# Layer 1's normalised batches turned by VectorE and DMAs instead of TensorE

## The chip, the core and the metric

The kernel runs on one core of one Trainium2 chip. Its engines work side by side, each through its own list of instructions in order: TensorE (PE in the profile; its weight loads are PEld) multiplies matrices into PSUM, VectorE (DVE), ScalarE (ACT) and GpSimd (POOL) work elementwise, SyncE (SP) issues most DMAs. An instruction that must wait for another engine or for a DMA waits on a semaphore, and everything behind it on its own engine waits with it. The metric is the device time of one execution in microseconds (us). Three runs of the kernel before gave 2046.7, 2047.1 and 2048.27.

## The reference, cut to what matters

The program computes two transformer layers on x of shape (4, 512, 512), each an attention and a feed-forward part (FFN) behind a layernorm that is scaled and shifted per batch. Layer 1, which the change concerns:

```python
h = _layernorm(x, axis=-1) * (1 + ca) + sa
x = x + ga * _L1_attn_ref(h, w_q, w_k, w_v, w_o)     # 32 heads of 128, 8 kv heads, causal
h = _layernorm(x, axis=-1) * (1 + cb) + sb
x = x + gb * _L1_ffn_ref(h, ...)                     # down(silu(gate(h)) * up(h)), 1792 wide, int weights with scales
```

`sa, ca, ga, sb, cb, gb` come from a small matrix product of a conditioning vector, one row per batch. The matmuls of both parts sum over the 512 features, and TensorE sums over partitions. The layernorm sums over features too, but is done with rows of x on the partitions. So the normalised x (rows on partitions) must be turned into h with features on partitions before it can be used. How it is turned is what the change is about.

## The kernel before, in words

Everything is fp32 or fp32r (P = 128, NT = 4 tiles of 128 rows a batch, KC = 4 chunks of 128 features, B = 4 batches, HKV = 8).

*Layer 0* comes first and is not touched. It ends near 205 us of the span.

*Attention of layer 1* runs over 32 blocks n, eight (g = 0 to 7) for each batch b. A block is two windows (`window`, lines 1120 to 1149), each with the scores, softmax and transposes of the eight tiles of the next pair of heads, the value products of the present pair, and a list of pieces, `fill`, which are dealt out over nine slots: products of the q, k, v and output projections, each as seven quarter products (`seven`, line 738). Two more lists, `side`, hold small work for the same slots. The order on every engine is written out by hand: what is issued first in the code stands first on its engine. `carry` (line 911) moves turned probabilities between partitions with 16 DMAs at the end of each window, on SP's queue; the value products read them in slots 8 and 9 of the next window.

A batch's x rests in DRAM (`x_d`). For the next batch (`after`) it is loaded in the odd window of block g = 4 into the one buffer `one_x`, and normalised in the even window of g = 5 by `norm_pieces` (line 995): VectorE takes the statistics, GpSimd the power -1/2 (`rstd`), VectorE `nmr`, and ScalarE scales the rows in place. In the odd window `turn_pieces` (line 1026) has TensorE turn four 128x128 squares a chunk into a PSUM bank (`lnT`, line 1035), and ScalarE scales, shifts and writes h1 (line 1038). Four empty pieces stand in the `fill` list of every odd window where a block has no turns (line 1263). `sums_h` then makes sums of h1 on GpSimd. The four h buffers `hp` hold h1 and its sums for two batches.

*The FFN* (`ffn_exact`, line 1281) runs over 4 batches of 14 steps n. In a step, `hidden` (line 1341) has TensorE compute gate and up (eight matmuls of 512 columns each, p_gate and p_up, line 1349), ScalarE take the sigmoid (line 1355), VectorE two products (1356, 1357), ScalarE the rounded half act_hi (122) and VectorE the rest act_lo (123). `down` (line 1363) then multiplies the halves of the step before into four accumulators (line 1368). Weights come in seven blocks, each of a gate, an up and a down part: `load` (line 1330) has SP load them into three rotating buffers wi and GpSimd cast them (line 1338), one block every second step of the first batch. The first batch also finishes what attention left: seven sums on GpSimd, four gates on VectorE (line 965) and four adds on GpSimd (line 969), three pieces a step from step 1 on. At step 8 the rows gb are loaded (`gates`, line 1051).

`prepare` (line 1294) makes the next batch's h in pieces, one a step from step 2: four statistics, the deviation (`ve`, `rstd`, `nmr`; line 63), two pieces of two normalised rows each (line 1306; into the room of attention's accumulator osum, called acc in the profile), and in steps 9 to 12 the four chunks: four transposes on TensorE into the bank `lnT` (line 1314), a scaling by VectorE (1318), and the two halves. The first batch's own h is made by `split_pieces` in attention's last windows, on TensorE.

[...]

Every DMA signals one of eight completion semaphores. They are given out in turn over all DMAs, whichever queue issues them, and a DMA isn't issued before the previous one on its semaphore has landed.

Of the kernel before, what the change touches and what calls it, by code (L numbers as in the profile page):

```python
# [8 lines left out]
F32 = mybir.dt.float32  # L9
# [8 lines left out]
P = 128  # L18
# [15 lines left out]
def adaln_two_layers(ctx: ExitStack, tc: tile.TileContext, a, out: bass.AP):  # L34
# [960 lines left out]
    def norm_pieces(xb):  # L995
# [7 lines left out]
        def xn(t):  # L1003
            nc.scalar.activation(
                xb[:, t, :], xb[:, t, :], AF.Identity,
# [19 lines left out]

    def turn_pieces(b, got):
# [3 lines left out]
        def piece(c):  # L1030
            if c == 0:
                h1[b] = hp.tile([P, KC, S], F32, tag="hT", name="hT")
            pt = bank([P, S], "lnT")
            for t in range(NT):
                nc.tensor.transpose(  # L1035
                    pt[:, t * P : (t + 1) * P], got["xn"][:, t, c * P : (c + 1) * P], ident
                )
# [4 lines left out]
            if c == KC - 1:  # L1042
                sums_h(b, (nc.gpsimd, nc.gpsimd))

        return [lambda c=c: piece(c) for c in range(KC)]
# [131 lines left out]
    begun = []  # L1177

    for n in range(NBLK):
# [17 lines left out]
        if g == HKV - 4:  # L1197
            xb = one_x()
            side[1] = get(after, xb)
        if g == HKV - 3 and after or n == NBLK - 2:  # L1200
            got, side[0] = norm_pieces(xb)
            if after:
                turns_ = turn_pieces(after, got)
# [12 lines left out]
        elif ahead:  # L1216
# [3 lines left out]
            else:  # L1220
                window(2 * n, begun[:2] + q[:2] + begun[2:] + q[2:], side[0], late)
                begun = []
                if 2 * (m + 1) < NBLK:
# [34 lines left out]
        else:  # L1258
# [4 lines left out]
            more = turns_ + 4 * [lambda: None]  # L1263
            window(2 * n + 1, o[:3] + now + more[:1] + o[3:4] + more[1:2] + o[4:5] + more[2:3] + o[5:6] + more[3:4] + o[6:], side[1], late)
# [16 lines left out]
    def ffn_exact():  # L1281
        with (
# [5 lines left out]
            tc.tile_pool(name="ps_tr2", bufs=1, space=PSUM) as ps_tr2,  # L1288
            tc.tile_pool(name="ps_hu", bufs=3, space=PSUM) as ps_hu,
# [4 lines left out]
            def prepare(b):  # L1294
# [3 lines left out]
                xn = osum.rearrange("p a b c -> p (a b c)")[:, : NT * E]  # L1298
                xn = xn.rearrange("p (t e) -> p t e", e=E)
# [4 lines left out]
                def norm(t):  # L1304
                    rstd, nmr = d["dev"]
                    nc.scalar.activation(
                        xn[:, t, :], x[b][:, t, :], AF.Identity,
                        bias=nmr[:, t : t + 1], scale=rstd[:, t : t + 1],
                    )
# [189 lines left out]
```

## Time and profile before

| what | value |
|---|---|
| three runs | 2046.7, 2047.1, 2048.27 us |
| profiled execution | 2046.79 us, of which the span from the first to the last instruction 2044.8 us |
| mean granted TensorE clock | 0.989 |
| TensorE busy | 2011.8 us, 98% |
| VectorE, ScalarE, GpSimd busy | 67%, 43%, 37% |
| TensorE waiting, all waits named | 1.8 us at most for any one cause after layer 0 but one (kT, 2.6 us) |
| first gate matmul of the FFN starts | 1727.53 us |

How to read it: the page gives busy time by engine; a group row has the line, engine, operation, tile written and tiles read, and durations. TensorE's durations contain a latency that the next matmul overlaps, so the distance of two starts is what a matmul costs. A wait row reads: engine, line that waited, what it waited for, total, times, longest. Rows in order of time begin with start and duration.

### The profile page before, as it was taken

The page shows a single profiled execution, that of the slowest core. Times are in us where ns is not written, and L with a number is a line of the kernel's source. Part 1 is how long each engine was busy: PE and PEld are TensorE (multiplying, and loading weights), DVE is VectorE, ACT ScalarE, POOL GpSimd, SP SyncE. Part 2 cuts the span into 40 slices and gives each one's busy share as a digit, 9 for nine tenths or more (in the row PEclk, how much of TensorE's full clock was granted, in tenths as well). Part 3 has the DMA queues.
Part 4 walks back from the last instruction along what each step waited for, and adds up shares of the span by engine and source line. Part 5 has one row for each costly group of instructions (what it writes and reads, how often), then busy time and mean ns, then how long its engine had stood idle before and what let it go on. Part 6 is the DMA issues. An engine that isn't in the chain of part 4 may idle for free.

```text
span 2044.8 us, 27496 instructions
## 1 busy us (share of the span) xinstructions
PE 2011.8 (98%) x9219; PEld 1573.9 (77%) x9219; DVE 1370.6 (67%) x3325; ACT 875.1 (43%) x1993; POOL 760.7 (37%) x659
## 2 busy tenths in 40 slices
PE   6999999999999999999999999999999999999998
PEld 4555777878787878777787878787877777888887
DVE  7767876677667766766677676667666675755554
ACT  4421644445444444544444445444444443323322
POOL 2316244334336433353473334337334333800000
PEclk8799999999999999999999999999999999999999
DMA  9222566665667766556776665567656556500000
GB/s 315 104 68 93 135 161 167 157 165 145 146 168 183 181 162 160 150 145 168 180 183 162 147 165 134 146 154 175 166 149 155 135 129 215 192 21 2 19 21 23
DMA packets 243640, 288.59 MB, mean 141 GB/s; under 512 B 23250, under 2 KB 184018, under 8 KB 243492
## 3 DMA queue, kind: packets, MB, share of 16 engines
q1 hardware_dynamic: 242964, 285.71, 53.2%
q8 instruction: 76, 1.25, 0.3%
q10 hardware_dynamic: 528, 1.05, 0.1%
q14 instruction: 72, 0.59, 0.1%
HBM read 142.99 MB, written 11.57 MB: 76 GB/s over the span
## 4 chain that ended last, share of the span: by engine, by line
PE 88%; DVE 1%; SPq 0%; DMA 0%; ACT 0%; issue 0%; DVEq 0%; ACTq 0%
PE quarter L746 46%; PE av L928 14%; PE sc L878 13%; PE p_gate L1349 5%; PE p_up L1349 5%; PE acc L1368 5%; PE lnT L1035 0%; PE lnT L1314 0%; DVE nmx L881 0%; SPq L918 0%; DMA x<-p 0%; DVE tm L1089 0%; DVE x L1377 0%; DVE tm L1376 0%; DVE p L896 0%
## 5 line engine op out<-in xcount | busy, mean ns | idle before, releaser
L878 PE MATMUL sc<-kT,qT 128*128 128x512 f32 (+3 forms) x1024 | 355.4, 433 | 0.8 <-DVE qT L778 0.8
L928 PE MATMUL av<-x,v 128*128 128x512 f32 x1008 | 292.1, 433 | 1.8 <-DMA x<-p 1.8
L928 PEld LDWEIGHTS av<-x,v 128*128 128x128 f32 x1008 | 188.4, 190 | 106.9 <-issue 62.4
L881 DVE TENSOR_REDUCE nmx<-sc 128x1 f32<-128x512 f32 (+3 forms) x512 | 251.6, 491 | 17.7
L893 ACT ACTIVATE x<-x,rden 128x512 f32<-128x512 f32 (+3 forms) x256 | 143.7, 561 | 239.3 <-DVE rden L892 239.3
L778 DVE TENSOR_TENSOR qT<-qT,quarter 128x512 f32<-128x512 f32 x224 | 150.6, 684 | 136.4 <-PE quarter L746 130.2
L893 ACT ACTIVATE p<-p,rden 128x512 f32<-128x512 f32 (+3 forms) x256 | 143.8, 562 | 223.2 <-DVE rden L892 221.7
L879 DVE TENSOR_TENSOR sc<-sc,mask 128x128 f32<-128x128 f32 x512 | 145.3, 284 | 133.1 <-PE sc L878 132.2
L842 DVE TENSOR_TENSOR acc<-acc,quarter 128x512 f32<-128x512 f32 x196 | 134.6, 687 | 131.4 <-PE quarter L746 131.3
L230 POOL TENSOR_TENSOR sq<-wq 128x512 f32<-128x512 f32 x32 | 41.1, 1286 | 474.0 <-DMA wq<-in_L_attn_w_q_dram 455.4
L878 PEld LDWEIGHTS sc<-kT,qT 128*128 128x128 f32 x1024 | 182.7, 191 | 25.5 <-DVE qT L778 1.2
L746 PEld LDWEIGHTS quarter<-wo,oT 128*128 128x128 f32 x744 | 140.9, 190 | 43.9 <-issue 20.1
L883 ACT ACTIVATE p<-sc,nmx 128x512 f32<-128x512 f32 (+3 forms) x256 | 135.1, 528 | 85.8 <-DVE nmx L881 77.2
L746 PE MATMUL quarter<-wo,oT 128*128 128x256 f32 x744 | 171.1, 379 | 0.2 <-ACT oT L933 0.2
L883 ACT ACTIVATE x<-sc,nmx 128x512 f32<-128x512 f32 (+3 forms) x256 | 134.9, 527 | 70.1 <-DVE nmx L881 65.4
L933 ACT COPY oT<-av 128x512 f32<-128x512 f32 x128 | 74.3, 580 | 162.1 <-PE av L928 160.2
L896 DVE STREAM_TRANSPOSE p<-p 128x512 f32<-128x512 f32 (+3 forms) x256 | 129.5, 506 | 1.8 <-ACT p L893 0.2
L896 DVE STREAM_TRANSPOSE x<-x 128x512 f32<-128x512 f32 x248 | 125.1, 504 | 1.4 <-ACT x L893 0.9
L746 PEld LDWEIGHTS quarter<-hT,wq 128*128 128x128 f32 x512 | 97.2, 190 | 32.5 <-issue 14.6
L746 PE MATMUL quarter<-hsum,sq 128*128 128x256 f32 x512 | 121.1, 379 | 0.0
L746 PE MATMUL quarter<-hsum,wq 128*128 128x256 f32 x512 | 121.0, 379 | 0.0
L746 PE MATMUL quarter<-hT,wq 128*128 128x256 f32 x512 | 120.9, 379 | 0.0
(257 smaller groups left out, 3749.4 us busy)
## 6 DMA issues: line engine op xcount, KB each, us to landing
x<-p SPq DMA_DIRECT2D x512, 128.0 KB, 3.7
x<-x SPq DMA_DIRECT2D x496, 128.0 KB, 3.8
wq<-in_L_attn_w_q_dram SPq DMA_DIRECT2D x32, 1024.0 KB, 5.9
wo<-in_L_attn_w_o_dram SPq DMA_DIRECT2D x31, 1024.0 KB, 5.6
wm<-in_L_wmod_dram SPq DMA_DIRECT2D x12, 1024.0 KB, 9.5
wk<-in_L_attn_w_k_dram SPq DMA_DIRECT2D x16, 512.0 KB, 4.0
wv<-in_L_attn_w_v_dram SPq DMA_DIRECT2D x16, 512.0 KB, 4.4
xn<-x_d SPq DMA_DIRECT2D x28, 256.0 KB, 5.6
```

The lines of the kernel that those rows point to most:

```text
L746: nc.tensor.matmul(ps[:, m, :], l[:, k, m * P : (m + 1) * P], r[:, k, :], start=(k == 0), stop=(k == 1),)
L778: nc.vector.tensor_tensor(c[out], c[v], ps, ADD if sign > 0 else SUB)
L842: nc.vector.tensor_tensor(osum[:, i - 1], osum[:, i - 1], ps, ADD)
L878: nc.tensor.matmul(ps[:, :w], q[:, i * P : w], kT[n][:, :w], start=True, stop=True)
L879: nc.vector.tensor_tensor(ps[:, i * P : w], ps[:, i * P : w], mask, ADD)
L881: nc.vector.tensor_reduce(nmx, ps[:, :w], AX.X, ALU.max, negate=True)
L883: nc.scalar.activation(blocks(s, i), ps[:, :w].rearrange("p (j q) -> p j q", q=BK), AF.Exp, bias=nmx, accum_out=den,)
L893: nc.scalar.mul(p, p, rden)
L896: nc.vector.transpose(blocks(s, i), blocks(s, i))
L928: nc.tensor.matmul(av.rearrange("p (a n) -> p a n", a=NG)[:, :, BK * k :], vs[n][:, k, :], pT[:, k, :, P * (s % 2) + BK * k : P * (s % 2 + ...
L1349: nc.tensor.matmul(ps[kind], w[kind][:, k, c * P : (c + 1) * P], h2[b % 2][i][:, k, :], start=(k == 0 and i == 0), stop=(k == KC - 1 and i ...
L1368: nc.tensor.matmul(acc[t], act[i][:, t * P : (t + 1) * P], w[:, c, :], start=(n == 0 and i == 0), stop=(n == NI - 1 and i == 1),)
```

## The change

In attention, for batches 1 to 3, the normalised rows are written in blocks of 32 columns (z, called xblocks), VectorE turns the 32x32 squares of such a block (four instructions of 512 columns a batch), and 16 DMAs on SP's queue move the turned squares to the partitions where they belong (y, called xturned), eight after the odd window of block g = 3, after its carry, and eight after the next even window. ScalarE then writes h1 from y. For this, x is loaded at g = 2 and normalised at g = 3. h1 is written in the odd window of g = 5, from the `side` list. The empty pieces in `fill` are gone. z and y use h buffers that are free at the time.

In the FFN, z and y lie in the room of osum. Two chunks are handled at a time (h = 0, 1): a normalised row is written in two halves, VectorE turns four blocks of 256 columns, and 16 DMAs for each half are issued by ScalarE, eight a step. Pieces begin at step 1, with two statistics a step. What attention left over is done at five pieces a step. The transposes' PSUM bank goes to gate and up. Layer 0 and the first FFN batch keep their transposes on TensorE.

```diff
+    TURN = [P, P // 32, NT, KC, 32]
+    def place_of(z, t):
+        return z[:, :, t], lambda ap: ap.rearrange("p (c j q) -> p j c q", j=P // 32, q=32)
+    def turn_blocks(z, j):
+        zj = z[:, j].rearrange("p t c q -> p (t c) q")
+        nc.vector.transpose(zj, zj)
+    def move_blocks(z, y, j, eng=nc.sync):
+        for i in range(P // 32):
+            eng.dma_start(y[32 * j : 32 * (j + 1), i], z[32 * i : 32 * (i + 1), j])
+    def chunk_of(y, c):
+        return y[:, :, :, c, :]
+    def in_order(ap):
+        return ap.rearrange("p (t i q) -> p i t q", t=NT, q=32)
...
     def turn_pieces(b, got):
-            pt = bank([P, S], "lnT")
-            for t in range(NT):
-                nc.tensor.transpose(
-                    pt[:, t * P : (t + 1) * P], got["xn"][:, t, c * P : (c + 1) * P], ident
-                )
             nc.scalar.activation(
-                h1[b][:, c, :], pt, AF.Identity,
+                in_order(h1[b][:, c, :]), chunk_of(got["y"], c), AF.Identity,
                 bias=m[:, 0, c, b : b + 1], scale=m[:, 1, c, b : b + 1],
             )
...
-        if g == HKV - 4:
+        if g == (HKV - 6 if after else HKV - 4):
             xb = one_x()
             side[1] = get(after, xb)
-        if g == HKV - 3 and after or n == NBLK - 2:
-            got, side[0] = norm_pieces(xb)
+        if g == HKV - 5 and after or n == NBLK - 2:
+            got, side[0] = norm_pieces(xb, after > 0)
             if after:
-                turns_ = turn_pieces(after, got)
+                turns_ = [lambda j=j: turn_blocks(got["z"], j) for j in range(P // 32)]
+        if g == HKV - 3 and after:
+            turns_ = turn_pieces(after, got)
...
+                run(*moves)
+                moves = []
...
-            more = turns_ + 4 * [lambda: None]
-            window(2 * n + 1, o[:3] + now + more[:1] + o[3:4] + more[1:2] + o[4:5] + more[2:3] + o[5:6] + more[3:4] + o[6:], side[1], late)
+            window(2 * n + 1, o[:3] + now + o[3:], turns_ + side[1], late)
+            if g == HKV - 5 and after:
+                moves = move_pieces(got)
+                run(moves.pop(0), moves.pop(0))
...
-            tc.tile_pool(name="ps_tr2", bufs=1, space=PSUM) as ps_tr2,
-            tc.tile_pool(name="ps_hu", bufs=3, space=PSUM) as ps_hu,
+            tc.tile_pool(name="ps_hu", bufs=4, space=PSUM) as ps_hu,
...
                 def norm(t):
                     rstd, nmr = d["dev"]
+                    for h in range(2):
+                        dst, read = place_of(z[:, h], t)
+                        nc.scalar.activation(
+                            dst, read(x[b][:, t, h * E // 2 : (h + 1) * E // 2]), AF.Identity,
+                            bias=nmr[:, t : t + 1], scale=rstd[:, t : t + 1],
+                        )
+                def turned_(h):
+                    for j in range(P // 32):
+                        turn_blocks(z[:, h], j)
+                def move(h, js):
+                    for j in js:
+                        move_blocks(z[:, h], y, j, nc.scalar)
                 def chunk(c):
+                    t = temp()
                     sc_, sh_ = m[:, 3, c, b : b + 1], m[:, 2, c, b : b + 1]
-                    nc.vector.tensor_scalar(t, pt, sc_, sh_, ALU.mult, ALU.add)
+                    nc.vector.tensor_scalar(
+                        in_order(t), chunk_of(y, c % 2), sc_, sh_, ALU.mult, ALU.add
+                    )
                     halves(h2[b % 2][0][:, c, :], h2[b % 2][1][:, c, :], t)
                 return (
-                    [lambda t=t: statistics(b, t, st, mv) for t in range(NT)] + [dev]
-                    + [lambda t=t: (norm(t), norm(t + 1)) for t in (0, 2)]
-                    + [lambda c=c: chunk(c) for c in range(KC)]
+                    [lambda: (stats(0), stats(1)), lambda: (stats(2), stats(3), dev())]
+                    + [lambda: (norm(0), norm(1)), lambda: (norm(2), norm(3), turned_(0), move(0, (0, 1)))]
+                    + [lambda: (move(0, (2, 3)), turned_(1)), lambda: None, lambda: chunk(0)]
+                    + [lambda: (chunk(1), move(1, (0, 1))), lambda: move(1, (2, 3))]
+                    + [lambda: None, lambda: chunk(2), lambda: chunk(3)]
                 )
...
-                    if n == 1 and b + 1 < B:
+                    if n == 0 and b + 1 < B:
                         ahead = prepare(b + 1)
...
-                    for _ in range(3):
+                    for _ in range(5):
                         if n > 0 and rest:
                             rest.pop(0)()
-                    if n > 1 and ahead:
+                    if n > 0 and ahead:
                         ahead.pop(0)()
```

`norm_pieces` with `blocks_` set writes its rows through `place_of` into z, and `move_pieces` makes four pieces of four moves each.

More of the change, by code (lines that the diff above doesn't have):

```diff
@@ L1024, in norm_pieces, with move_pieces, piece @@
         return out_, side + after
+    def move_pieces(got):
+        def piece(j):
+            if j == 0:
+                got["y"] = hp.tile(TURN, F32, tag="hT", name="xturned")
+            move_blocks(got["z"], got["y"], j)
+        return [lambda j=j: piece(j) for j in range(P // 32)]
     def turn_pieces(b, got):
```

36 lines of the change are left out of this document (21 added, 15 removed).

## The prediction

> **What bounds the kernel now.** I read the page's chain of waits first, then the instructions of the tile lnT (what the change removes), then the waits of each engine's queue, then the order of time at the start of the FFN. All times are in us from the span's start.
>
> ```profile
> PE 88%; DVE 1%; SPq 0%; DMA 0%; ACT 0%; issue 0%; DVEq 0%; ACTq 0%
> ```
>
> The end is set by TensorE; no other engine holds more than 1%. Between 209 and 1690 it is busy 1479.15 of 1481.00. So a matmul taken out is time gained, but only as long as nothing that feeds TensorE comes late.
>
> ```profile
> L1035 PE MATMUL lnT<-ident,xn x48: 272/273/273, 475.6 to 1249.5; 128*128 128x128 f32 x48
> ...
> L1314 PE MATMUL lnT<-ident,acc x48: 270/272/273, 1780.7 to 1954.8; 128*128 128x128 f32 x48
> ```
>
> The 272 ns are latency; transposes that follow each other start 0.109 apart, in the FFN as in attention.
>
> ```profile
> 1777.10 1.98 PE L1349 MATMUL p_up<-h,up 128*128 128x512 f32 x8
> 1778.91 0.39 PE L1368 MATMUL acc<-down,act_hi 128*128 128x512 f32 x1
> ...
> 1780.73 0.60 PE L1314 MATMUL lnT<-ident,acc 128*128 128x128 f32 x4
> 1781.08 2.08 PE L1349 MATMUL p_gate<-h,gate 128*128 128x512 f32 x8
> 1783.00 1.30 PE L1349 MATMUL p_up<-h,up 128*128 128x512 f32 x5
> ```
>
> One FFN step: gate 1.81, up 1.81, down of the step before 1.81, together 5.44. From one p_up to the next it is 5.90 here: four transposes cost 0.45.
>
> ```profile
> 1740.75 1.05 POOL L1338 CAST down<-wi 128x1024 fp32r<-128x1024 int32 x1 [0.67 <-DMA wi<-in_L_ffn_down_wqT_dram]
> 1741.76 1.29 POOL L972 TENSOR_TENSOR acc<-acc 128x512 f32<-128x512 f32 x1
> 1743.01 1.74 POOL L973 TENSOR_TENSOR acc<-acc 128x512 f32<-128x512 f32 x1
> ...
> 1755.50 1.75 POOL L969 TENSOR_TENSOR x<-x,acc 128x512 f32<-128x512 f32 x1
> 1757.19 1.51 POOL L1338 CAST gate<-wi 128x1024 fp32r<-128x1024 int32 x1
> ```
>
> GpSimd in order of time has no gap here: until 1757.19 it casts weights and does what attention left over. Then who waited for whom, in us in total, times, longest, of VectorE (1727 to 1800) and of SP's queue:
>
> ```profile
> DVE nmr L70 <- POOL rstd L68: 1.1, 1, 1.1
> ```
>
> ```profile
> SPq L208 <- PE quarter L746: 561.1, 59, 11.8
> ...
> SPq L990 <- DMA x<-x_d: 3.6, 8, 0.9
> ```
>
> VectorE waits for GpSimd's rstd at nmr. And an issue can wait for a DMA that it has no data from (x<-x_d for x<-x_d): all DMAs take eight completion semaphores in turn, whatever their queue, and each waits until the one eight before it has landed. Last, what an issue costs:
>
> ```profile
> L299 ACTq DMA_DIRECT2D x<-in_L_attn_x_dram x1: 472/472/472, 0.7 to 0.7; - x1
> ...
> L918 SPq DMA_DIRECT2D x<-p x512: 585/603/1803, 219.9 to 1691.5; - x171
> ```
>
> **The change, part by part.** The sum is against the profiled execution's 2046.79 (span 2044.8); the median 2047.1 lies 0.3 above.
>
> *Attention, removed:* 48 transposes at 0.109 = 5.2, all on the path. Their 12 ScalarE evictions (0.77) stay, reading xturned instead of PSUM (the nearest ScalarE row from SBUF is 0.80).
>
> *Attention, added:* 12 VectorE turns of 512 columns, one per slot of a window; L896's same shape takes 0.71, in all 8.5. VectorE is busy 1025 of 1481 and after layer 0 the PE waits name it for under 5 us in all. Also 48 moves on SP, each at most the carry's 0.60 row: 4.8 for a group of eight. They stand behind a window's carry and ahead of the next scan and k/v loads. SP waits 561 in 59 pieces (9.5 each) for TensorE to free a weight buffer, so the group fits; without that cover the next carry would be 4.8 late, and the value matmuls wait for it (once, 1.8 now). The x_d loads and statistics move two blocks earlier; their users come two blocks later. The odd windows' fill is spread evenly (2,1,1,1... pieces in place of 2,2,2,1,1,0,1,0,1): same work, nothing. I take 0; between -1 (fewer PSUM banks held) and +5 (one late carry per batch).
>
> *FFN, removed:* 12 chunks at 0.45 = 5.4. The fourth hu bank frees nothing that any wait names: 0.
>
> *FFN, first batch: order.* (Times stay in the clock of before; all of it happens 5.2 earlier.) The leftovers of attention (seven GpSimd sums, four VectorE gates, four adds) come five a step instead of three, statistics two a step, one step earlier. So in step 2 VectorE gets two gates, four statistics instructions, ve and nmr, ahead of step 3's gate product; GpSimd gets rstd behind seven sums, three casts and one add. Step 3's product (L1356, at 1745.06 before) now waits for nmr. The profile shows when GpSimd is through: that same work ends at 1757.19. With VectorE waiting, the 1.74 rows should fall towards 1.29, so I take 1756.3. Add rstd 1.02 (1757.3), nmr 0.16, two products 0.75 each, act_hi 0.62, act_lo 0.69: 1760.2. TensorE asks for act_lo at 1751.56 (down of step 3, second matmul). **Stall 1: 8.6** (7.8 to 10, with all sums at 1.29 or at 1.74). Queued behind rstd on GpSimd are three adds and the casts of weight block 4, ready at 1768; step 8 wants them after 1785, so that costs nothing.
>
> *Stall 2.* ScalarE next normalises into the osum region, by half rows (0.45, the 256-column ScalarE row). The second half row overwrites what the adds read, so it waits for the fourth add: behind act_lo (1760.2) two gates at 1.52 to 1.78 (1763.5) and an add 1.3 (1764.8). Three half rows (1766.2), then the sigmoid that stands behind them 0.69, products 1.5, hi, lo: 1769.7. TensorE, going on at 1760.2 with 1.6 of down and 3.6 of gate and up, asks at 1765.6. **4.1.**
>
> *Stall 3.* Four half rows end at 1770.9, then eight moves on ScalarE. Its sixth must wait for the load of gate block 6, which shares its semaphore. That load waits for the cast of block 5, that one for its own load, issued when block 4 is cast at 1765.9; a gate load takes 3.8 to land: 1769.7, cast 1770.8, load landed 1774.8. Three more issues (1776.2), sigmoid, products, hi, lo: 1779.8, against 1775.2. **4.6.**
>
> *Stall 4.* In the next group four moves share semaphores with the four gb rows, which SP issues after dsb, which waits for the load of up block 6. Up 5 was issued at 1766.9; an up load takes 5.1: landed 1772.0, cast behind gate 5 and so done by 1773.6, up 6 issued there, landed 1778.7. Issues of 0.52 end at 1781.3, landing takes 3.2 to 6.7 by the tile's own row; I take 5, near the middle: 1786.3. Then sigmoid to lo as before, 1790.6, against 1785.3. **5.3** (3.5 to 7). Sum of the four: 22.6.
>
> *FFN, later groups.* Each of the other five pairs of groups puts 2 x 8 issues on ScalarE ahead of two sigmoids. From the step's start: act_hi ends at 5.2, half rows 1.9, eight issues, sigmoid, products, act_hi 2.8, eight issues, sigmoid to act_lo 3.5: 13.4 + 16 issues. TensorE asks at 3 x 5.44 + 3.86 = 20.2: in time at 0.42 an issue, 1.6 late for each 0.1 more. ScalarE's only DMA row is 0.472 (a 1 MB load); SP's small or isolated ones are 0.27 to 0.33 plus 0.05 between; the carry's, back to back, 0.65 apart. I take 0.45, nearest to the first and second: 5 x 0.5 = 2.5; ends 0 and, at 0.65, 18. VectorE's 24 turns of 256 columns (0.44 by L896) follow act_lo, in steps where it has about 2 us free: 0.
>
> *Sum:* 2046.8 - 5.2 - 5.4 + 22.6 + 2.5 = 2061.3, with the median's 0.3: **2062**.
>
> [...] Transposes start 0.109 apart here and the fp32 shape on VectorE is 0.71 for four 32-row blocks abreast. [...] By the rows, moving the work alone is a gain of 10.6, since TensorE is full and VectorE is not (2036.5); the loss comes from the order. [...]
>
> **Rivals.**
> 1. *Everything added is hidden* (other side): TensorE gains 10.6, 2036.5. It needs nmr of step 2 before 1748, so GpSimd through its sums 8 us sooner than its row; for it speaks only that TensorE waits almost nowhere now. Against it: engines wait in order, and the nmr row shows VectorE waiting at this very place.
> 2. *Only stalls 1 and 2*: the loads have landed when ScalarE comes to its moves (ScalarE is late itself, and loads could run ahead if GpSimd catches up). 2062 - 9.9 = 2052.
> 3. *An issue on ScalarE is as dear as the carry's 0.65*: later groups 18 instead of 2.5, 2078. For it: 32-row moves back to back, like the carry; against it: a quarter of its rows.
> 4. *The attention half also loses* a late carry per batch: 2067.
> 5. *The change does less than it says:* the transposes of batch 0 before the FFN and of layer 0 stay on TensorE in any case; that is in the sum.
>
> **How the numbers follow.** This kernel's times can be told apart from about 0.2% (4 us). Forecast 2057 to 2069: 0.52. Rival 2: 0.15; rival 3: 0.14; rival 4: 0.09; rival 1: 0.10. The range 2049 to 2079 leaves out rival 1 and a tail of 0.05 on each side of rivals 2 and 3. Faster: rival 1, 0.09. Same (2043 to 2051): 0.06, the low side of rival 2. Slower: 0.85.
>
> **What would show it.** TensorE idle of about 20 between 1745 and 1795, in four pieces, put down to act_lo or act_hi; VectorE waiting some 6 for rstd; ScalarE's moves waiting for wi and gb loads; no lnT rows after 209 but those of one batch near 1690. Attention should end about 5 earlier. I am wrong if steps 4 to 7 of the first batch stay near 5.44, if the issue row on ScalarE is far from 0.45, or if the loss lies in attention windows.

## The result and the profile after

The changed kernel takes 2078.59 us in the median (2071.27 to 2079.6) against 2047.68 for the kernel before in the same comparison (four runs each): a ratio of 1.0149, 95% interval 1.0122 to 1.0175. It is 31 us slower. The profiled execution took 2079.6, with a span of 2077.8 and a mean clock of 0.984.

Executions of every kernel here fall into two groups about 9 us apart that differ in the granted clock (e1_attn_only: 2031.4 to 2034.0 at a mean of 0.992 to 0.997, 2039.4 to 2044.4 at 0.987 to 0.990; the profiles before and after, both of the longer group, have 41.0 and 47.8 us of layer 0 at half clock), and the share of each group moves medians from chip to chip. So besides ratios I use two lengths from the traces. *Attention* runs from its first quarter product to the first gate matmul of the FFN. *FFN* runs from that gate matmul to the last down matmul; the length of one of its batches is the distance from its first gate matmul to that of the next batch.

| kernel | median us | attention | FFN | its batches 0, 1, 2 |
|---|---|---|---|---|
| before | 2047.68 | 1544.05 | 312.00 | 76.8, 78.0, 78.0 |
| after | 2078.59 | 1538.97 | 347.91 | 102.2, 82.9, 83.7 |

Attention has become 5.1 shorter and the FFN 35.9 longer: 25.4 in batch 0, 4.9 and 5.6 in batches 1 and 2. The last batch prepares nothing and takes the same time in both. Layer 0 was 2.0 longer in the profile after (185.45) than in that of before (183.48). That is not the change: one and the same kernel shows both lengths (e1_attn_only 183.79, e10_attn_again 185.58).

The chain of waits of the changed kernel, which was 88% TensorE before:

```profile
PE 81%; DVE 4%; ACT 1%; DMA 1%; ACTq 1%; POOL 1%; issue 1%; SPq 0%; DVEq 0%; POOLq 0%
```

VectorE, ScalarE, its queue and GpSimd have entered it. TensorE's waits from 1720 to the end (engine, line, what it waited for: total, times, longest):

```profile
PE acc L1429 <- ACT act_hi L146: 26.5, 12, 9.0
PE acc L1429 <- DVE act_lo L147: 2.6, 12, 0.2
PE p_gate L1410 <- DVE acc L866: 0.9, 1, 0.9
```

The first two were 0.6 and 0.2 in the whole kernel before. The down matmuls wait for the activations of their step. The third row is new and belongs to the first gate matmul.

What holds the activations up is seen on the other engines. VectorE in order of time, in steps 2 and 3 of the first batch (start, duration, what ended the idle time before):

```profile
1744.50 1.76 DVE L989 TENSOR_TENSOR acc<-acc,ga 128x512 f32<-128x512 f32 x1 [2.55 <-POOL acc L999]
...
1747.91 0.26 DVE L66 TENSOR_SCALAR ve<-bnmv 128x4 f32<-128x4 f32 x1
1753.80 1.22 DVE L70 SCALAR_TENSOR_TENSOR nmr<-bnmv,rstd 128x4 f32<-128x4 f32 x1 [5.63 <-POOL rstd L68]
1754.94 0.74 DVE L1417 SCALAR_TENSOR_TENSOR tm<-p_gate,gus,tm 128x512 f32<-128x512 f32 x1
```

ve is there at 1748.2, but nmr starts 5.63 after VectorE is free, and the products of step 3 stand behind it. GpSimd in the same stretch shows why:

```profile
1750.32 1.26 POOL L1002 TENSOR_TENSOR acc<-acc 128x512 f32<-128x512 f32 x1
1751.53 1.25 POOL L993 TENSOR_TENSOR x<-x,acc 128x512 f32<-128x512 f32 x1
1752.75 1.01 POOL L68 TENSOR_TENSOR rstd<-ve,mhalf 128x4 f32<-128x4 f32 x1
```

rstd stands behind the last two of the seven sums and the first add. Then ScalarE, in order of time, first in the first batch and then in a later group (ACTq rows are DMA issues, the count at the end):

```profile
1757.09 0.60 ACT L1356 ACTIVATE acc<-x,nmr,rstd 128x256 f32<-128x256 f32 x1
1761.53 1.59 ACT L1356 ACTIVATE acc<-x,nmr,rstd 128x256 f32<-128x256 f32 x3 [3.84 <-POOL x L993]
1763.02 0.67 ACT L1416 ACTIVATE tm<-p_gate,gus 128x512 f32<-128x512 f32 x1
...
1767.98 6.45 ACTq L135 DMA_DIRECT2D acc<-acc  x8
1774.48 0.69 ACT L1416 ACTIVATE tm<-p_gate,gus 128x512 f32<-128x512 f32 x1 [6.52 <-DMA acc<-acc]
...
1777.63 6.68 ACTq L135 DMA_DIRECT2D acc<-acc  x8
1784.36 0.69 ACT L1416 ACTIVATE tm<-p_gate,gus 128x512 f32<-128x512 f32 x1 [6.90 <-DMA acc<-acc]
...
1856.17 5.01 ACTq L135 DMA_DIRECT2D acc<-acc  x8
1861.22 0.69 ACT L1416 ACTIVATE tm<-p_gate,gus 128x512 f32<-128x512 f32 x1 [5.07 <-PE p_gate L1410]
```

The second half row waits 3.84 for an add on GpSimd. The first two groups of eight moves take 6.45 and 6.68. A group in a later batch takes 5.01, or 0.63 an issue, although no load is left that it could wait for. In each case the sigmoid of the step stands behind them (the row at 1861.22 names p_gate, which was done at 1856, before the moves). The moves by themselves:

```profile
L135 ACTq DMA_DIRECT2D acc<-acc x96: 513/602/1464, 1768.0 to 1976.1; - x96
L135 SPq DMA_DIRECT2D xturned<-xblocks x48: 564/589/705, 407.0 to 1197.2; - x48
```

An issue of 32 rows takes 0.602 on ScalarE (1 KB rows) and 0.589 on SP (2 KB rows) in the median; the carry's issues on SP, 128 KB from 32 partitions, took 0.603 in the kernel before. So the bytes of a row made no difference here (0.589 to 0.603). The prediction took 0.45 with what lies between two issues.

The last view has TensorE by stretches (length, busy time and instructions, granted clock, DMA share, GB/s).

```profile
1748.00:1752.00 4.00, 0.26 (x2) 1.00 0.89 260
1752.00:1756.00 4.00, 0.00 (x0) 0.69 0.35 133
1756.00:1760.00 4.00, 2.76 (x6) 0.50 0.01 2
1760.00:1764.00 4.00, 4.00 (x12) 0.53 0.08 18
1764.00:1768.00 4.00, 3.83 (x16) 1.00 1.01 316
...
1788.00:1790.00 2.00, 2.00 (x6) 0.50 0.04 13
```

TensorE waits from 1748.1 to 1757.2. In that wait its granted clock falls to 0.50, and it stays there for 6.5 us of work: matmuls start 0.427 apart in place of 0.227. It is 0.50 again for 3.4 us behind each of the 5.4 and 2.7 us waits of stalls 3 and 4, and 1.00 behind the 1.4 us waits of later groups. From the gate matmuls of step 4 to those of step 5 it is 16.65, and the next three steps take 7.38, 12.62 and 10.05, in place of 5.44: 11.2, 1.9, 7.2 and 4.6 too much, 24.9 in all. (A piece done in step n holds up the products of step n + 1, and TensorE asks for these in step n + 2.)

### The profile page after: what moved, and what is told of

Same layout as the page of the kernel before. It is cut to its first block, busy times and chain, and to the rows that moved or that the text cites. A ratio compares the mean times of both kernels' runs of the same rounds, so it can differ in the third digit from the quotient of the medians.

```text
span 2077.8 us, 27503 instructions
## 1 busy us (share of the span) xinstructions
PE 2017.8 (97%) x9123; PEld 1572.8 (76%) x9123; DVE 1362.3 (66%) x3361; ACT 876.1 (42%) x2005; POOL 755.7 (36%) x659
## 4 chain that ended last, share of the span: by engine, by line
PE 81%; DVE 4%; ACT 1%; DMA 1%; ACTq 1%; POOL 1%; issue 1%; SPq 0%; DVEq 0%; POOLq 0%
PE quarter L770 46%; PE av L952 13%; PE sc L902 13%; PE acc L1429 3%; PE p_gate L1410 3%; PE p_up L1410 3%; ACTq L135 1%; DVE tm L1418 1%; DVE tm L1417 1%; ACT act_hi L146 1%; DVE act_lo L147 1%; SPq L942 0%; ACT tm L1416 0%; DMA acc<-acc 0%; DMA wi<-in_L_ffn_up_wqT_dram 0%
## 5 line engine op out<-in xcount | busy, mean ns | idle before, releaser
L902 PE MATMUL sc<-kT,qT 128*128 128x512 f32 (+3 forms) x1024 | 360.3, 434 | 0.8 <-DVE qT L802 0.8
L866 DVE TENSOR_TENSOR acc<-acc,quarter 128x512 f32<-128x512 f32 x196 | 134.2, 685 | 132.6 <-PE quarter L770 132.4
```

The costliest lines, as they stand in the source:

```text
L866: nc.vector.tensor_tensor(osum[:, i - 1], osum[:, i - 1], ps, ADD)
L902: nc.tensor.matmul(ps[:, :w], q[:, i * P : w], kT[n][:, :w], start=True, stop=True)
```

## The experiments

All lengths in us, as defined above; "before" and "after" stand in the table above.

| kernel | ratio to before (95%) | attention | FFN | batches 0, 1, 2 |
|---|---|---|---|---|
| e1_attn_only | 0.9968 (0.9946 to 0.9990) | 1537.01 | 312.17 | 77.0, 78.0, 78.0 |
| e10_attn_again | 0.9964 (0.9942 to 0.9985) | 1536.82 | 312.34 | |
| e2_ffn_only | 1.0168 (1.0125 to 1.0211) | 1545.35 | 345.06 | 99.1, 83.8, 83.0 |
| e3_sp_moves | 1.0003 (0.9979 to 1.0028) | 1537.72 | 318.54 | 87.1, 76.2, 76.2 |
| e4_order_b0 | 1.0155 (1.0114 to 1.0196) | 1539.38 | 348.45 | 101.4, 83.9, 84.0 |
| e5_busy | one run | 1538.41 | 320.92 | 89.5, 76.2, 76.2 |
| e7_four | one run | 1537.81 | 331.42 | 95.0, 79.1, 78.2 |
| e8_stats_first | one run | 1539.31 | 317.68 | 86.2, 76.2, 76.2 |
| e6_best | 0.9985 (0.9963 to 1.0007) | 1538.16 | 311.16 | 79.6, 76.3, 76.2 |
| e9_three | 0.9990 (0.9970 to 1.0010) | 1538.23 | 312.90 | 81.5, 76.2, 76.2 |
| e11_best | 0.9931 (0.9907 to 0.9955) | 1536.79 | 307.16 | 75.6, 76.3, 76.2 |

**The two halves apart (e1, e10, e2).** e1 takes the attention part of the diff alone and keeps the whole of `ffn_exact` as before; e2 takes the FFN part alone. e10 is e1 again on another chip.

> The change in attention alone; the FFN is that of the kernel before. Theory A (the attention half is a plain gain: 48 transposes at 0.109 less on TensorE, all that is added hidden): 2047.7 - 5.2 = 2042.5, TensorE 5.2 earlier at the end of attention than at its start. Rival R1 (the later start of attention in the profile after, 185.45 against 183.48, belongs to the change): 2045, with layer 0 again 2 to 2.6 later. Rival R2 (a late carry per batch, rival 4 of the prediction): 2052.

> The change in the FFN alone; attention is that of the kernel before. Theory A (the FFN half is the whole loss): the FFN 348 long instead of 312, 2047.7 + 36 = 2083, with the same four stalls in steps 4 to 7 of the first batch. Rival R3 (the stalls come from the attention half, which leaves work or transfers over for the FFN): the four stalls are gone or changed, 2060 or less.

The attention half is a gain of 7.0 (1544.05 to 1537.01, again 1536.82), at a ratio of 0.997. The FFN half is the whole loss: 345.06 long, with four stalls in the same steps (9.9, 1.9, 7.7 and 1.4 over 5.44; the fourth was 4.6 in the whole change). R1, R2 and R3 are refuted. The gain is 1.8 more than the 5.2 of the transposes. TensorE by stretches near the end of attention shows where that is, first in the kernel before:

```profile
1696.00:1698.00 2.00, 1.39 (x4) 0.66 1.04 381
1698.00:1700.00 2.00, 2.00 (x6) 0.50 1.08 352
```

and the same place in e1_attn_only, some 5 earlier:

```profile
1692.00:1694.00 2.00, 2.00 (x11) 1.00 1.09 372
1694.00:1696.00 2.00, 2.00 (x12) 1.00 0.64 203
```

Both kernels have the same three waits there, 0.2, 1.2 and 0.7 long, the longest for a softmax (pT for p). Before, 3.4 us at half clock followed; in e1 none did. So that part of the gain is not work taken out, and no run shows what decides it. The whole change has it too, with a granted clock of 1.00 from 197.0 to 1753.5, and nothing in the change was meant to bring it.

**ScalarE's queue (e3).**

```diff
-                        move_blocks(z[:, h], y, j, nc.scalar)
+                        move_blocks(z[:, h], y, j, nc.sync)
```

> All of the change, but the FFN's moves are issued by SP instead of ScalarE. Theory A (ScalarE's sequencer is what is short: 0.625 an issue, eight ahead of a sigmoid, and the waits for the loads' semaphores held on it): the nine later groups cost nothing (-18), of the stalls of the first batch the third and fourth go with what they cost in clock (-11), the first stays: 2050. Rival R4 (the moves land late whoever issues them, so VectorE waits for them at the chunk's tensor_scalar, and the loads stand behind them on SP): only the later groups are gained, 2061 or more. Rival R5 (the groups cost what they do through VectorE's turns, not through the issues): 2078, no change.

One word takes back 29.4 of the FFN's 35.9. Batches 1 and 2 run through at 76.16, which is 1.88 less than before: all that four chunks of transposes were worth. In batch 0 the third and fourth stalls are gone. What TensorE still waits for in e3_sp_moves from 1720 on:

```profile
PE acc L1429 <- ACT act_hi L146: 9.8, 3, 8.5
PE p_gate L1410 <- DVE acc L866: 0.9, 1, 0.9
PE acc L1429 <- DVE act_lo L147: 0.4, 2, 0.2
```

and SP in order of time:

```profile
1765.31 10.38 SPq L135 DMA_DIRECT2D acc<-acc  x16
```

Sixteen issues take 10.38 there, 0.65 each: SP pays no less than ScalarE. It has nothing behind them that TensorE needs soon. R4 is refuted (VectorE waits once, 2.6, for a move), and R5 too: the turns are the same and cost nothing. The expectation of 2050 was met with 2048.04.

**Four issues a step (e7).** ScalarE's queue as in the change, but four moves a step.

```diff
+                four = [[lambda j=j, h=h: move(h, (j,)) for j in range(P // 32)] for h in range(2)]
                 return (
-                    [lambda: (stats(0), stats(1)), lambda: (stats(2), stats(3), dev())]
-                    + [lambda: (norm(0), norm(1)), lambda: (norm(2), norm(3), turned_(0), move(0, (0, 1)))]
...
+                    [lambda: (stats(0), stats(1), stats(2), stats(3), dev()), lambda: (norm(0), norm(1))]
+                    + [lambda: (norm(2), norm(3), turned_(0), four[0][0]())] + four[0][1:3]
+                    + [lambda: (four[0][3](), turned_(1)), lambda: chunk(0)]
+                    + [lambda: (chunk(1), four[1][0]())] + four[1][1:]
+                    + [lambda: (chunk(2), chunk(3))]
```

In this kernel the half rows of batch 1 are written in step 2, over sums that the last leftovers of attention still read in step 3, so those are computed from other numbers; the work is the same in kind and amount. Its first batch starts otherwise than that of the change and is not used.

> All of the change, ScalarE's queue kept, but four moves a step instead of eight in every batch (one piece more a batch). Read in the second and third batch, which take 84.1 and 84.6 for 14 steps in the profile after (83.9 and 84.6 from gate to gate), 76.2 without a stall. Theory A (eight issues of 0.625 stand ahead of a sigmoid and are 1.4 too long for it; four, 2.5, are not): 76.2 each, so some 16 less; the whole 2063, with the stalls of the first batch much as they are. Rival R9 (each issue costs its part whatever its group, because TensorE's slack is used up by any of them): half of the gain at most, 80 each. Rival R10 (the moves land too late for the chunks now): new stalls at the chunks, 82 or more.

Batches 1 and 2 take 79.1 and 78.2 in place of 82.9 and 83.7: 9.3 of the 14.3 that they had over 76.16 are gone. ScalarE in a later batch:

```profile
1846.79 2.44 ACTq L135 DMA_DIRECT2D acc<-acc  x4
1849.28 0.69 ACT L1417 ACTIVATE tm<-p_gate,gus 128x512 f32<-128x512 f32 x1 [1.87 <-DMA acc<-acc]
```

Steps with four moves and nothing else are 5.44 long; an issue still costs 0.61, so it is the length of the group that decides, as theory A said. Theory A's 76.2 was not reached: the 2.9 and 2.0 that are left lie, but for 0.4 at the start of batch 1, behind two pieces of each batch, into which all four statistics, and half rows with turns and four moves, had been put together. R9 is refuted by the steps of 5.44, though its 80 is not far from 79.1; R10 (82 or more) is refuted too.

**The order of the first batch (e4, e8).** e4 gives the first batch the old pace: leftovers three a step, statistics one step later.

```diff
-                    if n == 0 and b + 1 < B:
+                    if n == (1 if b == 0 else 0) and b + 1 < B:
...
-                    for _ in range(5):
+                    for _ in range(3):
...
-                    if n > 0 and ahead:
+                    if n > (1 if b == 0 else 0) and ahead:
```

Here too the first half rows (step 4) are written over sums that the last leftovers (step 5) still read, and these are computed from other numbers; the work is the same in amount.

> All of the change, but in the first batch the order of the kernel before: the leftovers of attention three a step, statistics from step 2 on. Theory A (the first stall is nmr behind GpSimd's sums and adds, held in front of the gate product; the third and fourth come from the loads and stay): the 9.0 wait and the half clock behind it go, 12 in all: 2066. Rival R6 (one late start causes all four; without it the loads are through before the moves): 2055. Rival R7 (the stall only moves with the statistics): 2078.

The FFN is no shorter (348.45). R7 is nearest: the stalls only change places. VectorE in e4_order_b0:

```profile
1744.16 0.98 DVE L70 SCALAR_TENSOR_TENSOR nmr<-bnmv,rstd 128x4 f32<-128x4 f32 x1 [4.83 <-POOL rstd L68]
```

and TensorE's waits from 1712 on:

```profile
PE acc L1429 <- ACT act_hi L146: 17.0, 11, 3.9
PE acc L1429 <- POOL down L1399: 7.1, 1, 7.1
...
```

One step later and three at a time, rstd still stands behind all seven sums: 4.83 in place of 5.63. GpSimd's sums, not the number of pieces a step, set when it comes. And a weight cast is late now, since on GpSimd it stands behind adds that wait for VectorE. So my edit did not test what I wanted. e8 takes the cause itself away: on the basis of e3, batch 1's statistics, rstd and nmr go into step 1, ahead of the leftovers.

```diff
+                    if b == 0 and n == 1:
+                        ahead.pop(0)()
+                        ahead.pop(0)()
                     for _ in range(5):
                         if n > 0 and rest:
                             rest.pop(0)()
-                    if n > 0 and ahead:
+                    if n > (2 if b == 0 else 0) and ahead:
```

> e3_sp_moves, with the statistics, rstd and nmr of batch 1 all in step 1 and ahead of what attention left over, so that rstd does not stand behind GpSimd's sums. Length of the FFN, 318.5 in e3_sp_moves. Theory A (stall 1 is that order; behind it lies a second wait, the half rows for the fourth add): no wait for rstd over 2, stall 1 gone (-12.4 with its clock), the half rows hold ScalarE until GpSimd's last add near 1755 and the down matmuls of step 4 come some 7 late, with half clock behind it: 315. Rival R11 (the half rows' wait is covered): 306. Rival R12 (VectorE is late with the statistics in step 1, and stalls there instead): a stall in step 2 or 3.

The wait for rstd falls from 5.6 to 1.1, but the FFN is only 0.9 shorter, 317.68. ScalarE in e8_stats_first:

```profile
1744.78 0.60 ACT L1356 ACTIVATE acc<-x,nmr,rstd 128x256 f32<-128x256 f32 x1 [5.37 <-DMA wi<-in_L_ffn_down_wqT_dram]
1748.91 1.58 ACT L1356 ACTIVATE acc<-x,nmr,rstd 128x256 f32<-128x256 f32 x3 [3.53 <-POOL x L993]
1750.40 0.67 ACT L1416 ACTIVATE tm<-p_gate,gus 128x512 f32<-128x512 f32 x1
```

The second wait, which was behind the first, is now the one that counts: the half rows stand on ScalarE until GpSimd's last add, and the sigmoid stands behind them. TensorE waits 7.2 for act_hi, as theory A had it (7). The expected 315 is missed by 2.7, of which 1.1 and 1.4 are in steps 3 and 4, where VectorE is late after the four statistics of step 1 and two gates of step 2 (R12 in part).

**A TensorE kept busy (e5).** On the basis of e3, the up matmuls of step 4 are issued five times over, so that most of the 8.64 us of stall 1 (8.5 in the row of waits, which counts from the end of a matmul's latency) is filled with work of no use.

```diff
-                for kind in ("gate", "up"):
-                    ps[kind] = ps_hu.tile([P, 512], F32, tag="hu", name=f"p_{kind}")
+                for kind in ("gate",) + (5 if (b, n) == (0, 4) else 1) * ("up",):
+                    if kind not in ps:
+                        ps[kind] = ps_hu.tile([P, 512], F32, tag="hu", name=f"p_{kind}")
```

> e3_sp_moves, with the up matmuls of step 4 of the first batch issued five times instead of once (32 matmuls more, 7.25 at 0.2267 each, in the place of most of the 8.64 that TensorE waits there). The numbers are for the length of the FFN, from its first gate matmul to its last down matmul (318.5 in e3_sp_moves). Theory B (half of what a long wait costs comes after it: TensorE, left without work, goes on at half the clock, and so the work put into the wait pays): the wait falls to about 1.4, the matmuls behind it start 0.227 apart at once: 315, 3.8 less for 32 matmuls more. Rival R8 (the matmuls behind the wait are slow for another reason, the loads or VectorE at the same memory): 318.5, and they start 0.427 apart as before.

The FFN is 320.92, longer by 2.4, so the forecast of 315 is wrong, and R8 as well. TensorE in e5_busy, in order of time:

```profile
1755.19 0.50 PE L1430 MATMUL acc<-down,act_hi 128*128 128x512 f32 x1 [1.98 <-ACT act_hi L146]
...
1756.26 0.40 PE L1430 MATMUL acc<-down,act_hi 128*128 128x512 f32 x1
1756.49 0.40 PE L1430 MATMUL acc<-down,act_lo 128*128 128x512 f32 x1
...
1764.10 0.47 PE L1430 MATMUL acc<-down,act_hi 128*128 128x512 f32 x1 [2.64 <-ACT act_hi L146]
```

and by stretches:

```profile
1758.00:1760.00 2.00, 2.00 (x11) 1.00 0.00 0
...
1762.00:1764.00 2.00, 0.00 (x0) 1.00 0.00 0
...
1766.00:1768.00 2.00, 2.00 (x6) 0.50 0.12 29
```

Theory B is right on the clock: behind a wait of 2.0 in place of 8.6 the matmuls start 0.23 apart at once, at clock 1.00. It is wrong on the gain. With TensorE at full speed, its next wait comes out, 2.64 at 1764.10 for step 4's act_hi, where there was 0.7 in e3. That act_hi hangs on ScalarE's half rows and GpSimd's adds, not on TensorE. Half clock had cost nothing there, because it ran beside that wait. Now the clock falls behind the second wait instead (0.50 from 1766 to 1768), where nothing covers it: if it lasts 3.4 us, as it did in the kernel before, that is 1.7 of the 2.4, by estimate. The other 0.7 would not be the clock's: in e5 GpSimd began its sums 14.1 after the first gate matmul, in e3 13.5, since a weight load landed later.

**Towards a version that is faster than both (e6, e9, e11).** All three issue the moves from SP, and change the first batch further.

e6 adds to e8: half rows of batch 1 in step 5, all sixteen moves of a half at once, in steps 5 and 9, and an unused tile in front of the hu banks.

```diff
+            spare = ps_hu.tile([P, 512], F32, tag="hu", name="spare")
...
+                if b == 1:
+                    return (
+                        [lambda: (stats(0), stats(1)), lambda: (stats(2), stats(3), dev())]
+                        + [lambda: None] * 2
+                        + [lambda: (norm(0), norm(1), norm(2), norm(3), turned_(0), move(0, range(4)))]
+                        + [lambda: turned_(1), lambda: None, lambda: chunk(0)]
+                        + [lambda: (chunk(1), move(1, range(4))), lambda: None, lambda: None]
+                        + [lambda: (chunk(2), chunk(3))]
+                    )
```

> e8_stats_first, with the half rows of batch 1 (and the first sixteen moves) only in step 5, behind the last add, the second sixteen moves in step 9; and a spare tile ahead of the first hu bank, so that the first gate matmul takes the bank that the kernel before gave it. Theory A: no stall left in the FFN, 306 long; attention to the first gate matmul 1537.0 as in e1_attn_only (1538.0 to 1539 in the others); against the median of before 2046.4 - 7 - 6 = 2033.5. Rival R13 (the moves land too late for the chunks of step 8 or 12, or the loads of blocks 5 and 6 behind them come late for steps 10 and 12): 2037 to 2042.

The wait for the adds is gone, and the FFN is 311.16; 306 was expected. What is left are four small stalls: 0.8, 1.4 and 2.1 in steps 3 to 5, where VectorE is late with statistics and with gates that are slow beside GpSimd's sums (in the kernel after a gate takes 1.76 and 1.77 beside them and 0.68 with GpSimd idle), and 0.8 at the start of batch 1, where block 0, which is loaded again, came late behind the moves on SP. The spare tile changed nothing in the wait at the start of the FFN.

e9 goes back to three leftovers a step, and puts all 32 moves behind the last weight load.

```diff
+            tc.tile_pool(name="ps_tr2", bufs=1, space=PSUM),
-            tc.tile_pool(name="ps_hu", bufs=4, space=PSUM) as ps_hu,
+            tc.tile_pool(name="ps_hu", bufs=3, space=PSUM) as ps_hu,
...
+                ys = [y, z[:, 0] if b == 1 else y]
...
+                        [lambda: (stats(0), stats(1)), lambda: (stats(2), stats(3), dev())]
+                        + [lambda: (norm(0), norm(1), norm(2), norm(3), turned_(0))]
+                        + [lambda: turned_(1), lambda: None]
+                        + [lambda: (move(0, range(4)), move(1, range(4))), lambda: None]
+                        + [lambda: chunk(0), lambda: chunk(1), lambda: (chunk(2), chunk(3))]
...
+                    if b == 0 and n < 2:
+                        ahead.pop(0)()
+                    for _ in range(3):
...
+                    if n > (4 if b == 0 else 0) and ahead:
```

> The version that the runs so far point to. Attention as in the change. FFN: moves from SP; for batch 1 what attention left over three pieces a step as in the kernel before, statistics in steps 0 and 1 ahead of it, half rows and turns in steps 5 and 6, all 32 moves in step 8 behind the last weight load (the second sixteen into the room that the first sixteen leave, not into that of the first chunks), chunks in steps 10 to 12; three hu banks and one left empty, as before. Theory A (nothing is left that makes TensorE wait): the FFN 305 to 306 long (312.0 before, 311.2 in e6_best), attention to the first gate matmul 1537 (1544.05 before), 13.5 less than before in all. Rival R14 (the moves land behind step 12, or block 6 is late): 308 to 311. Rival R15 (the 1.14 at the start of the FFN is not a matter of the bank): 1538 to 1539 for attention.

> The kernel of e1_attn_only on the chip of e9_three. Theory A: 7 less than before, and 6.5 more than e9_three.

e9 misses again, at 312.90, and so does what was expected beside e10: by the lengths e10 is 2.0 shorter than e9, not 6.5 longer. TensorE's waits in e9_three from 1700 on:

```profile
PE p_up L1420 <- DVE tm L1427: 4.5, 1, 4.5
PE p_gate L1420 <- DVE acc L866: 0.9, 1, 0.9
...
```

Half rows in step 5 still waited 4.1 for the last add, the turns on VectorE waited 4.5 for them, the products stood behind the turns, and with three banks TensorE had no room left for its next result. The wait at the start stayed too, as if a pool that holds no tile kept no bank. e11 mends these points:

```diff
+            tc.tile_pool(name="ps_up", bufs=1, space=PSUM) as ps_up,
-            tc.tile_pool(name="ps_hu", bufs=4, space=PSUM) as ps_hu,
+            tc.tile_pool(name="ps_hu", bufs=3, space=PSUM) as ps_hu,
...
+                        [lambda: (stats(0), stats(1)), lambda: (stats(2), stats(3), rstd_()), nmr_, lambda: None]
+                        + [lambda h=h: ([norm(t, (h,)) for t in range(NT)], turned_(h)) for h in range(2)]
+                        + [lambda: (move(0, range(4)), move(1, range(4))), lambda: None]
+                        + [lambda: chunk(0), lambda: chunk(1), lambda: (chunk(2), chunk(3))]
...
+                    room = ps_up if kind == "up" and n % 2 else ps_hu
+                    ps[kind] = room.tile([P, 512], F32, tag="hu", name=f"p_{kind}")
...
+                    if n > (3 if b == 0 else 0) and ahead:
```

> e9_three mended in three places: nmr apart from rstd and only in step 4, the half rows one step later and ordered by halves (first halves and their turns in step 6, second halves in step 7), and the PSUM banks as in the kernel before at the start of the FFN (three hu banks at the old place, the fourth, in front of them, only for the up result of odd steps). Theory A: the waits for rstd (2.3), for the last add (4.1) and for the bank (4.5, with half clock behind it) are gone, the FFN 305 to 306 long (312.0 before); the first gate matmul waits for nothing, attention 1537 (1544.05 before); 13.5 less than before in all, 6.5 less than e1_attn_only. Rival R14 (the second sixteen moves land behind step 12): 308 to 311. Rival R15 (the 1.14 at the start of the FFN is no matter of the bank): 1538.

The ratio is 0.9931 (0.9907 to 0.9955), with a median of 2027.37 against 2046.79 on the same chip. By the lengths it is 12.1 shorter than before (1536.79 and 307.16 against 1544.05 and 312.00), and 5.2 shorter than e1. Of the 12.1, 1.8 is the half clock that the kernel before met near 1697. TensorE's waits in e11_best from 1700 on:

```profile
PE acc L1450 <- ACT act_hi L146: 0.6, 1, 0.6
PE p_gate L1431 <- POOL gate L1419: 0.4, 1, 0.4
PE quarter L770 <- ACT oT L957: 0.2, 1, 0.2
...
```

The wait at the start of the FFN (the L866 row of the others; 1.14 from start to start) is gone with the bank, so R15 is refuted. 307.16 lies 1.2 over the expected 305 to 306: at the start of batch 1 the gate weights of block 0, loaded again behind the moves, are late (the second row, 0.4; the two steps around it are 0.75 too long), and step 6 is 0.3 too long.

## Why the prediction was wrong in size

The direction and the four stalls were right, the time was not: 2062 was forecast, 2078.59 was measured. The step that failed is "FFN, later groups", where an issue on ScalarE was taken at 0.45: 2.5 was forecast for it, 17.0 was measured, at 0.60 an issue and 0.63 from one to the next. That is also one of the signs of being wrong that the prediction named (an issue row far from 0.45). Point by point:

- *Attention, removed: 5.2, and added: 0.* Right for e1, which has 7.0, of which 1.8 is the half clock near 1697 that e1 did not meet. That the whole change shows 5.1 is chance: there 1.1 of the bank (below) and a stretch of half clock at 193.6 to 197.0 (granted 0.50) stand against the 7.0. No carry is late: TensorE waits for it once, 1.8 in e1, as before.
- *FFN, removed: 12 chunks at 0.45.* Right: 1.88 a batch in e3 (1.80 forecast).
- *"The fourth hu bank frees nothing that any wait names: 0."* Wrong by 1.1. The bank did not free anything, but the four banks reach into the room of attention's projections, and the first gate matmul waits until VectorE has read the last of these (the L866 row, 0.9). e11 shows it by putting the bank elsewhere.
- *Stalls 1 to 4: 8.6, 4.1, 4.6, 5.3, in sum 22.6.* The sum is 24.9, and the places and causes are right: in stall 4, for one, the chain of waits runs 4.0 through the landing of a gb row before the last moves go out. The trace before shows the turn of the semaphores: its 1313 issues use eight of them strictly in turn, and of the 821 on the five whose landings are all recorded none starts before the previous one on its semaphore has landed. In the trace after, the sixth move, issued at 1772.64, has the semaphore of the gate load issued at 1767.63, and four moves of the next group, issued from 1780.12 on, have those of the four gb rows issued from 1776.06 on. The single sizes are not, and that the sum comes so near is in part chance. TensorE waits 9.0 in the first, nearly the 8.6. But it goes on at half clock, the next step takes 1.9 longer, and the wait that was to be stall 2, 4.1, shrinks to 0.2 under that cover; e5 brings 2.6 of it to light. Stalls 1 and 2 together are 13.1 against 12.7. Stalls 3 and 4 are 11.8 against 9.9; of those, 5.4 and 2.7 are waits, and the rest is mostly half clock, for which the prediction had no term.
- *Later groups: 2.5 at p = 0.45.* Measured 2.7 for the second pair of batch 0, 6.8 in batch 1 and 7.5 in batch 2: 17.0. The working itself, 13.4 + 16 p against 20.2, holds: with 5.01 / 8 for p it gives 3.2 for a pair, and the five took 2.7 to 4.1. (At 0.45 it gives 0.4 for a pair; the prediction wrote 0.5.) Only p was mis-sized, by the choice of its row. I had rows of wide or single DMAs, one of them ScalarE's own, and the carry's, whose issues look like the moves: 32 rows, back to back. I took the former for the nearest. The carry's row was the right one: that a move is a quarter of its size counted for nothing (0.602 and 0.603 an issue), and in e3 the engine made no difference (0.65 an issue on SP, 0.63 on ScalarE). The range's far end, 18, was this case.
- *Rivals.* The third, an issue as dear as the carry's, gave 2078 and is what happened in the later groups. That its time is met to 0.6 is partly chance: 17.0 in place of 18 and the 1.8 of half clock that attention no longer met stand against 2.3 more of stalls, 1.1 of the bank and a layer 0 that was 2.0 longer. The first (all hidden, 10.6 less than before) did not, but e11, the same work in another order and queue, is 12.1 shorter, or 10.3 without the 1.8 of half clock. The fourth is refuted by e1; the second by the ACTq rows, where moves do wait for loads, on ScalarE itself: 6.45 and 6.68 in place of 5.01.

The prediction took from the rows that moving the work alone is a gain. e11, with the turns on VectorE and a ratio of 0.9931, agrees: on this TensorE, 98% busy, transposes were a loss even at 0.109 each.

What stays open: no run moved the waits near 1695 on purpose, so how the 1.8 comes about is not shown.

## What to carry to other kernels

Price a DMA issue by the row that is like it in shape and sequence, not by the engine that issues it, and count a group of issues as one block of that engine's time: eight of 0.63 in front of a sigmoid cost 0.7 to 2.1 a group, four cost nothing, and on a queue with nothing urgent behind them sixteen cost nothing. Before moving work earlier, look at what stands ahead of it on each engine that it passes; when you take one such wait away, the next one on the list takes its place, as e4, e8 and e5 showed, and only after the last had been cleared was the FFN 4.8 us shorter than before. Where half clock followed uncovered, a wait on TensorE was worth more than its length: the 2.7 in stall 4 cost 4.6.

## What the runs showed of the hardware that I had not expected

After a wait of 9.1, 5.4 or 2.7 us in the changed kernel, TensorE went on at a granted clock of 0.50, matmuls 0.427 apart in place of 0.227, for up to 6.5 us; after waits of 1.4 us in the later groups it did not (1.00). Yet shorter waits were enough elsewhere: one of 2.6 in e5 (0.50 at 1766 to 1768), and in the kernel before two of 1.2 and 0.7 close together (0.50 at 1698 to 1700).

The traces of the kernels before and after give the clock by stretches. Between 180 us and the last instruction, those at half clock are one of 3.41 us in the former (from 1696.65), and four in the latter: 3.41 from 193.60, 10.24 from 1753.49, 3.41 from 1777.39 and 3.41 from 1787.63. The last three start 23.90 and 10.24 apart, seven and three times 3.41. In the 3.41 us ahead of a stretch of half clock TensorE was busy 1.52 in the former, and, in order of time, 1.40, 0.00, 0.00 and 0.89 in the latter. It was busy hardly more, 1.59, from 1746.67 to 1750.08 in the latter, and the clock stayed at 1.00 for the next 3.41. In e5 it was 1.00 behind the wait of 2.0 and 0.50 behind the one of 2.6. What decides was not tested.

VectorE was at times slower in GpSimd's company. In the kernel after, two gates of the leftovers took 1.76 and 1.77 beside GpSimd's sums and a third 0.68 with GpSimd idle, but the fourth, most of it beside an add, 0.68 as well; nmr, an instruction of 128x4, took 1.22 beside an add and 0.16 with GpSimd idle.

In e5 a wait and the half clock behind it did not add, as something else was late too: 32 matmuls of no use in a wait of 8.64 kept the clock at 1.00 and won nothing.
